# A block of two gated cross attentions on one Trainium2 core: the mask matmuls of the second attention write only their own keys, and the last keys' mask travels with the negated maximum

## The chip, the cores and the metric

The kernel runs on one core of a Trainium2 chip, as one program. TensorE (PE) multiplies matrices and writes its results to PSUM, which has eight banks; VectorE (DVE), ScalarE (ACT) and GpSimd (POOL) do the rest of the arithmetic; SyncE (SP) mostly issues transfers. Each engine works through its own instruction queue in order, and waits for the others through semaphores. The metric is the device time of one execution, in microseconds (us). A profile of one execution shows when each instruction ran.

## The reference

The input `x` has 4 batches of 1024 tokens with 256 channels; the context has 4 batches of 77 keys. Four layers follow each other, each added to `x` with a gate: a cross attention, a mixture of experts, a second cross attention with 16 heads of 16 channels, and a self attention over the 1024 tokens in two classes of tokens. The second cross attention, which the change touches, is

```python
energy = jnp.einsum('bqhd,bkhd->bhqk', q, k)             # q from the normed x, k and v from the context
energy = jnp.where(mask, energy, jnp.float32(-1e+20))    # mask: 1 x 1 x 1024 x 77, the same for every batch and head
attn = jax.nn.softmax(energy / np.sqrt(HEAD), axis=-1)
out = jnp.einsum('bhqk,bkhd->bqhd', attn, v).reshape(N, Lq, EMBED)
return out @ Wo.T + bo
```

The last layer normalises queries and guides, splits tokens into two classes by a similarity (`sim > 0.9` after scaling with the minimum and the maximum over all batches and tokens), and lets each token attend to the keys of its own class.

## The kernel before

There are two stages. The first holds everything up to the end of the second cross attention, and also the queries, keys and values of the last layer, which go to memory as `q_d`, `k_d` and `v_d`. The second is the attention of the last layer: 16 units (4 batches by 4 groups of heads), in which the scores' maxima (`ps_m` L1649, `nm` L1656), the scores (`sc` L1685, `p` L1693) and the weighted sums (`av` L1703) run interleaved. Its order is written out by hand.

The order of the first stage is made by `Plan`. Each step is added with an estimated cost for every engine that may run it, the steps it comes after, the ring buffers it takes and those it gives back. `Plan.run` then builds the program greedily: of all steps whose predecessors are done it takes the one with the least start plus lateness, where the start is worked out from the estimated costs, and it chooses the engine where there is a choice (ACT or DVE for most copies out of PSUM). The table `LATENESS` gives the lateness of some steps, by name and engine. So a changed cost moves not only its own step: it can move every later one, on every queue. The projections to keys (`keys_of`, through `store`, L695) and values (`values_of`, L711) of the last layer carry a lateness of 300, and so fill gaps of PE.

The second cross attention is `by_heads(b, m)`: one call for each pair of token tiles (256 tokens), 16 calls in all. The four row groups of 32 partitions (`r`) hold two heads each in either half of the channels (`c`), and each row group has its own PSUM bank. A call does, among other things:

- `score` (L1046 and L1056), once for each of the two tiles: into four banks of 128 tokens by 308 columns (4 heads by 77 keys) go the mask first, and then the products of queries and keys. The mask is laid down by matmuls whose stationary operand is `bias1_t`, the transposed mask values (0, or minus 2^100) of 32 keys; the moving operand `key_of` says which key each of the 32 rows stands for. There are three blocks of keys (32, 32 and 13), so three matmuls for each of the four banks, and each of the twelve writes all 308 columns.
- `greatest_` (L1069): DVE takes the negated maximum over the keys of each head.
- `split` (L1086 to L1089) and `turn_parts` (L1094): the negated maxima are split into a high and a low bf16 part and turned into rows, 8 of the 32 in each row group; the others are zero. `parts_out` copies them from PSUM to `nmt` as bf16, on ACT or DVE (L238).
- `score_t` (L1121), once for each half of the channels: the transposed scores, 77 keys by 256 tokens, in four banks. Five matmuls accumulate in each place: the product of keys and queries, the three blocks of the mask, and the negated maximum (`pick2` by `nmt`).
- `exps` (L1126), `weigh1` (L1133), the denominators' way through memory (`den`, `inv_d`, `rin`, L1172 to L1190), the division, the output projection (L1199), and then for the last layer a layer norm, `queries` (L1234), a power on POOL (L1280) and the storing of the queries.

`store` splits its result in two (a copy to `stage`, L238, and the rest by DVE, L671) and sends it to memory; `stage` has two buffers. After the last call `classes_by_token` finds the minimum and the maximum of `sim` and the classes (L1312 to L1377), and `prepare` fetches the rows of the first unit (L206), for which POOL blanks the buffers once batch 0 and batch 1 no longer use them (L1403, L1407).

The masks are made ready once, near the start, by `masks` (L566) and turned by L578; `picks` (L597 to L603) builds `key_of` and `pick2`.

Of the kernel before, what the change touches and what calls it, by code (L numbers as in the profile page):

```python
# [19 lines left out]
P = 128  # L20
# [28 lines left out]
class Plan:  # L49
# [22 lines left out]
        ("split", "DVE", 0): 150,  # L72
        ("<lambda>", "DVE", 0): 150,
        ("k_rows", "POOL", 1500): 300,
        ("parts_out", "ACT+DVE", 0): 600,
        ("sums_", "DVE", 1000): 0,
        ("all_rows", "DVE", 0): 0,
        ("q_rows", "POOL", 0): 1000,
# [81 lines left out]
def block_kernel(ctx: ExitStack, tc: tile.TileContext, t_in: dict, out: bass.AP):  # L160
# [57 lines left out]
    with ExitStack() as abc:  # L218
# [288 lines left out]
        def head_weights():  # L507
# [55 lines left out]


            def masks(_):
                ve.tensor_scalar(bias1[:, :, 0:S2], mask1, -1.0, BIG, ALU.add, ALU.mult)  # L566
                ve.tensor_copy(ident_h, ident)

            masked = work_on(masks, {DVE: 750}, ["mask1"])
# [24 lines left out]
            def picks(_):  # L594
                fold = small.tile([P, 32], F32, name="fold", bufs=1)
                col = small.tile([P, J], F32, name="pick_c", bufs=1)
                ve.tensor_reduce(fold, ident.rearrange("p (r k) -> p k r", r=J), AX.X, ALU.add)  # L597
                for q in range(3):
                    n = min(32, S2 - 32 * q)
                    ve.tensor_copy(key_of[:, q, 32 * q : 32 * q + n], fold[:, 0:n])  # L600
                ve.tensor_reduce(col, fold[:, 0 : 2 * J].rearrange("p (n e) -> p n e", e=2), AX.X, ALU.add)
                ve.tensor_copy(pick2, bc(col, 2, S2))
                ve.tensor_reduce(mine16, fold.rearrange("p (i d) -> p i d", d=D), AX.X, ALU.add)  # L603

            done.append(work_on(picks, {DVE: 1200}, []))
# [415 lines left out]
        def by_heads(b, m, after, reads):  # L1021
# [15 lines left out]
            for i in range(2):  # L1037


                def score(_, i=i):  # L1040
                    at_ = (2 * m + i) * P
                    banks = g2["s", i] = [bank("ps_e", [P, J * S2]) for r in range(4)]
                    for q in range(3):
                        for r in range(4):
                            rows32 = slice(32 * r, 32 * r + 32)
                            pe.matmul(  # L1046
                                banks[r],
                                bias1_t[rows32, q, at_ : at_ + P],
                                bc(key_of[rows32, q], 1, J),
                                start=q == 0,  # L1050
                                stop=False,
                            )
                    for c in range(2):
                        for r in range(4):
                            rows32 = slice(32 * r, 32 * r + 32)
                            pe.matmul(  # L1056
                                banks[r][:, c * 2 * S2 : (c + 1) * 2 * S2],
                                xt[rows32, c, i * P : i * P + P],
                                kb1[rows32, b, c],
                                start=False,  # L1060
                                stop=c == 1,
                            )

                def greatest_(_, i=i):
                    if i == 0:
                        g2["nm"] = small.tile([P, 2, J, J], F32, name="nm2", bufs=2)
                    for r in range(4):
                        by_head = g2["s", i][r].rearrange("p (n k) -> p n k", k=S2)
                        ve.tensor_reduce(g2["nm"][:, i, r], by_head, AX.X, ALU.max, negate=True)  # L1069

                i1 = plan.add(score, {PE: 1180}, [xt_at] + weights[2], take=["bank"] * 4)
                users.append(i1)
                tops.append(
                    plan.add(
                        greatest_, {DVE: 1620}, [i1, *tops], take=[] if i else ["nm2"], give=[("bank", i1)]
                    )
                )
# [17 lines left out]

            def parts_out(e):
                g2["nmt"] = tmp.tile([P, NQ], BF16, name="nmt", tag="nmt", bufs=plan.size["nmt"])
                copy(e, g2["nmt"], g2["ps_nm"])

            i2 = plan.add(split, {DVE: 600}, tops, take=["parts"], give=[("nm2", tops[0])])  # L1100
            i3 = plan.add(turn_parts, {PE: 300}, [i2], take=["bank"], give=[("parts", i2)])
            i4 = plan.add(parts_out, both(375, 430), [i3], take=["nmt"], give=[("bank", i3)])
            heads = []
            for c in range(2):

# [2 lines left out]
                def score_t(_, c=c):  # L1108
                    banks = g2["st", c] = [bank("ps_st", [S2, 2, NQ]) for r in range(4)]
                    at_ = 2 * m * P  # L1110
                    for i in range(2):
                        for k in range(5):
                            for r in range(4):
                                rows32 = slice(32 * r, 32 * r + 32)
                                if k == 0:
                                    of = kb1[rows32, b, c, i], xt[rows32, c, :]
                                elif k < 4:
                                    of = key_of[rows32, k - 1], bias1_t[rows32, k - 1, at_ : at_ + NQ]
                                else:
                                    of = pick2[rows32, 2 * c + i], g2["nmt"][rows32]  # L1120
                                pe.matmul(banks[r][:, i, :], *of, start=k == 0, stop=k == 4)  # L1121

                def exps(_, c=c):
                    p = g2["p", c] = act.tile([S2, 4, 2, NQ], F32, name="pt", tag="pt", bufs=plan.size["pt"])
# [18 lines left out]
                def weigh_out(e, c=c):  # L1143
                    copy(e, g2["raw"][:, :, c, :], g2["av", c])

                i5 = plan.add(score_t, {PE: 1920}, [i4], take=["bank"] * 4)
                i6 = p_at = plan.add(exps, {ACT: 2000}, [i5], take=["pt"], give=[("bank", i5), ("nmt", i4)])
                i7 = plan.add(
                    weigh1,
# [892 lines left out]
```

## Time and profile before

| | |
|---|---|
| median of 3 runs | 1187.44 us (1185.3 to 1190.38) |
| the profiled execution | 1189.9 us, its span 1188.2 us |
| instructions | 28427 |
| PE busy | 1148.5 us (97%) |
| DVE busy | 1003.2 us (84%) |
| ACT busy | 942.4 us (79%) |
| POOL busy | 610.0 us (51%) |
| mean granted TensorE clock | 0.988 of full speed |

Busy times are unions of the instructions' spans on an engine. Matmuls are pipelined and their recorded spans overlap, so 97% does not mean that PE works at its peak; how much room PE takes up is better read from the distance between the starts of one matmul group and the next. One fp32 matmul shows as two records. A group line gives the operation, its shapes, how often it ran, busy time and mean duration, and then the idle time just ahead of it with what ended it. The chain of waits goes back from the last instruction to what released it at each step. The first stage ends, and the second begins with the first `ps_m`, between 420 and 445 us.

### The profile page before, as it was taken

The numbers are of one execution on the slowest core, as the hardware profiler recorded it, in microseconds if no ns is written. First come the engines' busy times: TensorE is split into PE (matmuls) and PEld (weight loads), VectorE is DVE, ScalarE is ACT, GpSimd is POOL, SyncE is SP. The second block draws the span as 40 slices with busy tenths as digits, with TensorE's granted clock in tenths as the row PEclk, the third lists the DMA queues.
The fourth block names the chain that finished last, engine by engine and source line by source line (L and its number), as shares of the span: only waits on it lengthen the run. The fifth ranks groups of instructions, "written<-read, shape, count | busy, mean of one in ns | idle before, by whom it ended". The sixth has DMA issues, their size and how long they took to land.

```text
span 1188.2 us, 28427 instructions
## 1 busy us (share of the span) xinstructions
PE 1148.5 (97%) x10524; PEld 626.1 (53%) x10524; DVE 1003.2 (84%) x2097; ACT 942.4 (79%) x1942; POOL 610.0 (51%) x691
## 2 busy tenths in 40 slices
PE   7999999999999989999999999999999999999998
PEld 5566776777766655444434344444344444344443
DVE  5899686686866469989999999899999899999984
ACT  4875568666666413989999999899999899999886
POOL 6454566567675631644444565443564444465531
PEclk9999999999999979999999999999999999999999
DMA  8000011111112767321123341123241123220011
GB/s 240 24 1 4 21 56 67 55 48 49 48 49 74 221 204 203 69 70 34 41 62 60 60 110 38 35 65 76 60 114 38 34 62 69 70 48 20 21 28 57
DMA packets 59589, 80.27 MB, mean 68 GB/s; under 512 B 17274, under 2 KB 42789, under 8 KB 59451
## 3 DMA queue, kind: packets, MB, share of 16 engines
q1 hardware_dynamic: 55242, 73.17, 23.0%
q0 software_dynamic: 2960, 4.19, 1.6%
q8 instruction: 83, 1.36, 0.5%
q10 hardware_dynamic: 1248, 1.10, 0.3%
q14 instruction: 56, 0.45, 0.1%
HBM read 47.39 MB, written 26.07 MB: 62 GB/s over the span
## 4 chain that ended last, share of the span: by engine, by line
PE 74%; DVE 12%; ACT 6%; DMA 3%; POOL 2%; issue 2%; SPq 1%; ACTq 0%; DVEq 0%; POOLq 0%
PE av L1703 19%; PE sc L1685 17%; PE ps_m L1649 8%; DVE nm L1656 6%; PE ps_st L1121 4%; ACT p L1693 3%; PE ps_av L1133 2%; PE ps_o L1199 2%; PE ps_q L1234 2%; PE ps_xt L781 2%; PE ps_y L990 2%; PE ps_o L1760 2%; PE ps_xb L886 1%; PE ps_rs L1579 1%; PE ps_e L1056 1%
## 5 line engine op out<-in xcount | busy, mean ns | idle before, releaser
L1656 DVE TENSOR_REDUCE nm<-ps_m 128x1 f32<-128x512 f32 x1024 | 633.0, 679 | 40.8 <-PE ps_m L1649 28.5
L1693 ACT ACTIVATE p<-sc 128x512 f32<-128x512 f32 x1024 | 541.5, 631 | 28.6 <-PE ps_m L1649 18.3
L1721 POOL TENSOR_TENSOR raw<-raw,part 128x512 f32<-128x512 f32 x213 | 272.2, 1278 | 351.9 <-ACT part L1720 340.5
L1649 PE MATMUL ps_m<-slot,slot 64*128 64x512 f32 x768 | 279.6, 450 | 2.0
L1703 PE MATMUL av<-p,v 128*32 128x512 f32 x2048 | 274.2, 607 | 0.5
L1685 PE MATMUL sc<-slot,slot 64*128 64x512 f32 x768 | 239.9, 430 | 8.6 <-ACT p L1693 5.4
L1685 PEld LDWEIGHTS sc<-slot,slot 64*128 64x128 f32 x768 | 123.8, 185 | 133.4 <-ACT p L1693 52.8
L1649 PEld LDWEIGHTS ps_m<-slot,slot 64*128 64x128 f32 x768 | 128.1, 184 | 47.2 <-ACT p L1693 32.0
L1720 ACT COPY part<-av 128x512 f32<-128x512 f32 x213 | 131.7, 619 | 21.2 <-PE av L1703 19.4
L1280 POOL TENSOR_TENSOR ss_all<-ss_all,mhalf 128x16 f32<-128x16 f32 x32 | 92.6, 2903 | 12.8 <-DVE ss_all L1251 12.8
L1649 PE MATMUL ps_m<-kt,qt 64*128 64x512 f32 x256 | 90.1, 460 | 1.7 <-DVE stage L671 1.0
L1685 PE MATMUL sc<-qt,kt 64*128 64x512 f32 x256 | 84.2, 435 | 1.8 <-DMA qt<-nmt 1.6
L1126 ACT ACTIVATE pt<-ps_st 77x512 f32<-77x512 f32 x128 | 64.2, 599 | 20.2 <-PE ps_st L1121 20.2
L1703 PEld LDWEIGHTS av<-p,v 128*32 128x32 f32 x2048 | 40.4, 108 | 72.7 <-ACT p L1693 40.9
L1685 PEld LDWEIGHTS sc<-qt,kt 64*128 64x128 f32 x256 | 42.9, 185 | 63.5 <-DVE nm L1656 35.2
L1069 DVE TENSOR_REDUCE nm<-ps_e 128x4 f32<-128x308 f32 x128 | 51.7, 469 | 14.3 <-PE ps_e L1056 14.3
L769 ACT ACTIVATE xnp<-x,shift_all,rstd_all 128x256 f32<-128x256 f32 x96 | 52.1, 605 | 11.8 <-POOL shift_all L748 9.3
L736 DVE BATCH_NORM_STATS2 bn_st<-x 128x6 f32<-128x256 f32 x128 | 51.5, 403 | 2.2 <-DMA x<-in_x 1.7
L1649 PEld LDWEIGHTS ps_m<-kt,qt 64*128 64x128 f32 x256 | 41.0, 188 | 19.7 <-ACT p L1693 8.8
L238 ACT COPY xt<-ps_xt 128x512 f32<-128x512 f32 (+1 forms) x57 | 31.7, 583 | 13.9 <-PE ps_xt L781 13.4
L745 POOL TENSOR_SCALAR rstd_all<-mv_all 128x2 f32<-128x2 f32 (+3 forms) x46 | 11.4, 247 | 59.6 <-DVE mv_all L737 47.6
L746 POOL TENSOR_TENSOR rstd_all<-rstd_all,mhalf 128x2 f32<-128x2 f32 (+3 forms) x46 | 39.3, 854 | 3.8
(324 smaller groups left out, 1722.8 us busy)
## 6 DMA issues: line engine op xcount, KB each, us to landing
slot<-k_d SPq DMA_DIRECT2D x72, 128.0 KB
slot<-q_d SPq DMA_DIRECT2D x72, 128.0 KB
q_d<-stage SPq DMA_DIRECT2D x32, 256.0 KB
k_d<-stage SPq DMA_DIRECT2D x16, 512.0 KB
v_d<-vs SPq DMA_DIRECT2D x16, 272.0 KB
v<-v_d SPq DMA_DIRECT2D x16, 272.0 KB
x<-in_x SPq DMA_DIRECT2D x8, 512.0 KB
rin<-inv_d SPq DMA_DIRECT2D x32, 128.0 KB
```

Of the source, the lines that this page charges most:

```text
L736: ve.bn_stats(st[:, i, :], X[b][:, t0 + i, :])
L769: se.activation(to[:, i, :], xb[:, t0 + i, :], AF.Identity, bias=shift[:, i : i + 1], scale=rstd[:, i : i + 1],)
L1069: ve.tensor_reduce(g2["nm"][:, i, r], by_head, AX.X, ALU.max, negate=True)
L1126: se.activation(p[:, r], g2["st", c][r], AF.Exp)
L1280: gp.tensor_tensor(ss, ss, mhalf.to_broadcast([P, H]), ALU.pow)
L1649: pe.matmul(ps, QT[u % SLOTS][r, i, t * P : t * P + P], KT[u % SLOTS][r, i, h * CH : h * CH + CH], start=True, stop=True,)
L1656: ve.tensor_reduce(nm[:, 2 * i + j // 2, t % (T // 2), h : h + 1], ps, AX.X, ALU.max, negate=True)
L1685: pe.matmul(ps, KT[u % SLOTS][r, i, t * P : t * P + P], QT[u % SLOTS][r, i, ch * CH : ch * CH + CH], start=True, stop=True,)
L1693: se.activation(p[j], ps, AF.Exp)
L1703: pe.matmul(ps[32 * j : 32 * j + 32, :], V_all[b % 2][:, at : at + 32], p[j], start=True, stop=True)
L1720: se.copy(part, ps)
L1721: gp.tensor_tensor(to, to, part, ALU.add)
```

## The change

- In `score`, each mask matmul writes only the columns of its own keys, in each of the four heads: 128, 128 and 52 columns instead of 308 three times. The cost that the plan is told goes from 1180 to 1000.
- In `score_t`, the third block of the mask is no longer a matmul of its own. The mask values of keys 64 to 76 are laid 16 columns further on, so that after the turn they stand in rows 16 to 28 of each row group, where `nmt` is zero. `parts_out` adds them to the negated maxima on the way out of PSUM, and `pick2` also holds `key_of` of the third block. One matmul then adds both. Four matmuls accumulate instead of five; the planned cost goes from 1920 to 1700.
- `parts_out` is now an addition of two tensors, for which the plan has DVE alone; the entry in `LATENESS` is renamed to match.
- `masks` takes two operations instead of one, and in `picks` a copy becomes an addition.

```diff
-        ("parts_out", "ACT+DVE", 0): 600,
+        ("parts_out", "DVE", 0): 600,
...
             def masks(_):
-                ve.tensor_scalar(bias1[:, :, 0:S2], mask1, -1.0, BIG, ALU.add, ALU.mult)
+                for of, to in ((slice(0, 64), slice(0, 64)), (slice(64, S2), slice(80, S2 + 16))):
+                    ve.tensor_scalar(bias1[:, :, to], mask1[:, :, of], -1.0, BIG, ALU.add, ALU.mult)
...
-                    ve.tensor_copy(key_of[:, q, 32 * q : 32 * q + n], fold[:, 0:n])
+                    ve.tensor_copy(key_of[:, q, 32 * q : 32 * q + n], fold[:, 16 * (q == 2) : 16 * (q == 2) + n])
...
-                ve.tensor_copy(pick2, bc(col, 2, S2))
+                ve.tensor_tensor(pick2, bc(col, 2, S2), bc(key_of[:, 2], 1, J), ALU.add)
...
                     for q in range(3):
+                        keys = slice(32 * q, min(32 * q + 32, S2))
                         for r in range(4):
                             rows32 = slice(32 * r, 32 * r + 32)
                             pe.matmul(
-                                banks[r],
+                                banks[r].rearrange("p (n k) -> p n k", k=S2)[:, :, keys],
                                 bias1_t[rows32, q, at_ : at_ + P],
-                                bc(key_of[rows32, q], 1, J),
+                                bc(key_of[rows32, q, keys], 1, J),
...
-                i1 = plan.add(score, {PE: 1180}, [xt_at] + weights[2], take=["bank"] * 4)
+                i1 = plan.add(score, {PE: 1000}, [xt_at] + weights[2], take=["bank"] * 4)
...
-                copy(e, g2["nmt"], g2["ps_nm"])
+                ve.tensor_tensor(g2["nmt"], g2["ps_nm"], bias1_t[:, 2, 2 * m * P : 2 * m * P + NQ], ALU.add)
...
-            i4 = plan.add(parts_out, both(375, 430), [i3], take=["nmt"], give=[("bank", i3)])
+            i4 = plan.add(parts_out, {DVE: 430}, [i3], take=["nmt"], give=[("bank", i3)])
...
-                        for k in range(5):
+                        for k in range(4):
...
-                                elif k < 4:
+                                elif k < 3:
                                     of = key_of[rows32, k - 1], bias1_t[rows32, k - 1, at_ : at_ + NQ]
                                 else:
                                     of = pick2[rows32, 2 * c + i], g2["nmt"][rows32]
-                                pe.matmul(banks[r][:, i, :], *of, start=k == 0, stop=k == 4)
+                                pe.matmul(banks[r][:, i, :], *of, start=k == 0, stop=k == 3)
...
-                i5 = plan.add(score_t, {PE: 1920}, [i4], take=["bank"] * 4)
+                i5 = plan.add(score_t, {PE: 1700}, [i4], take=["bank"] * 4)
```

## The prediction

> **What bounds the kernel now.** I read four views: the page, a table by stage, the chain of waits in the stretch that the change touches, and the timelines of PE and SP there. From the page (busy time, share, instructions) and the table (columns: length, busy time and instructions of PE, PEld, DVE, ACT, POOL, granted clock, DMA share, GB/s):
>
> ```profile
> PE 1148.5 (97%) x10524; PEld 626.1 (53%) x10524; DVE 1003.2 (84%) x2097; ACT 942.4 (79%) x1942; POOL 610.0 (51%) x691
> ```
> ```profile
> 90.00:385.00 295.00, 290.08 (x3756) 209.96 (x3749) 217.25 (x597) 199.78 (x438) 184.54 (x204) 0.99 0.15 47
> 385.00:431.00 46.00, 43.17 (x164) 28.52 (x163) 21.96 (x57) 16.13 (x33) 26.25 (x25) 0.96 0.74 225
> 431.00:444.00 13.00, 11.33 (x28) 6.98 (x27) 9.32 (x15) 2.82 (x6) 5.33 (x5) 0.61 0.51 173
> 444.00:1188.00 744.00, 726.10 (x6119) 326.13 (x6116) 685.49 (x1223) 665.27 (x1334) 343.53 (x358) 1.00 0.26 62
> ```
>
> All calls of the second cross attention lie in 90:385. PE is covered for 290 of 295 us there, DVE for 217 (74%), ACT for 200. From 385 to 444 transfers matter too (DMA share 0.74, then 0.51). The 744 us after that are the last layer, untouched: they move as a block with their start. Shares of the chain within 90:385, by line:
>
> ```profile
> by line: PE ps_st L1121 16.3%; PE ps_av L1133 10.0%; PE ps_o L1199 8.0%; PE ps_q L1234 7.0%; PE ps_y L990 6.9%; PE ps_xt L781 6.4%; PE ps_e L1056 3.9%; PE ps_e L1046 3.9%; PE ps_y L991 3.4%; PE ps_xb L886 2.9%; DVE nm L1069 2.8%; DMA rin<-i
> ```
>
> L1121 is 48.1 us of the chain and L1046 11.5: the shortened matmuls are on it. Nearly every step there is PE's own queue, so PE bounds this stretch. The tail, from SP's timeline and the chain (start, length):
>
> ```profile
> 410.88 3.73 SPq L206 DMA_DIRECT2D kt<-k_d  x6
> ...
> 416.65 22.09 SPq L679 DMA_DIRECT2D k_d<-stage  x8
> ```
> ```profile
> 398.30 1.74 PE ps_o L1199 x8
> ...
> 430.79 0.74 PE ps_m L1649 x2
> ...
> 444.02 2.48 DVE nm L1656 x4
> ```
>
> The last output projection ends at 400.0; the last layer's first matmul starts at 430.8. Between them eight key stores go out one every 2.76 us, and DVE's queue waits behind their `stage` copies.
>
> **The change, part by part.** Everything is set against the profiled execution (span 1188.2, 1189.9 us); its differences go onto the median, 1187.4, which is 2.5 below it. The rows used (PE's timeline; then groups with busy time and mean ns; L578 with ns min/median/max and first and last start):
>
> ```profile
> 196.15 0.61 PE L1121 MATMUL ps_st<-xt,kb 32*77 32x256 f32 x8
> 196.58 0.51 PE L1121 MATMUL ps_st<-bias_t,key_of 32*77 32x256 bf16 x12
> 196.90 0.29 PE L1121 MATMUL ps_st<-nmt,pick 32*77 32x256 bf16 x4
> 197.01 0.61 PE L1121 MATMUL ps_st<-xt,kb 32*77 32x256 f32 x8
> ```
> ```profile
> 202.23 0.59 PE L1046 MATMUL ps_e<-key_of,bias_t 32*128 32x308 bf16 x12
> 202.65 0.69 PE L1056 MATMUL ps_e<-kb,xt 32*128 32x154 f32 x16
> ```
> ```profile
> L1056 PEld LDWEIGHTS ps_e<-kb,xt 32*128 32x128 f32 x496 | 18.6, 184 | 1.1
> L238 ACT CAST nmt<-ps_nm 128x256 bf16<-128x256 f32 x10 | 3.7, 371 | 5.4 <-PE ps_nm L1094 5.4
> L238 DVE CAST nmt<-ps_nm 128x256 bf16<-128x256 f32 x6 | 2.5, 410 | 0.4 <-PE ps_nm L1094 0.4
> ```
> ```profile
> L578 PE MATMUL ps_bias<-ident_h,room x96: 219/219/229, 32.9 to 34.2; 128*32 128x128 bf16 x96
> ```
>
> *Scores by key (L1121).* From start to start, three mask groups take 196.90 - 196.58 = 0.32 us, so one takes 0.107. Sixteen calls, two halves, two tiles: 64 groups go, 6.9 us of PE.
>
> *Scores by token (L1046).* Twelve matmuls take 202.65 - 202.23 = 0.42 us. Now they stream 128, 128 and 52 columns. Floor: L578 streams 128 columns in four groups side by side, 96 matmuls starting within 1.3 us, 13.7 ns each; twelve take 0.16 and save 0.26. Ceiling: each group waits for its own weights, and the one that follows is fp32 with 0.184 of loading; then about 0.39 remain and 0.03 is saved. I take two groups at L578's pace and about 0.12 for the third, because the fp32 load starts behind it: 0.24, saving 0.18. Times 32: 5.8 us (ends 1.0 and 8.2).
>
> [...]
>
> PE loses 12.7 us in all (7.9 to 15.1).
>
> *Negated maxima (L238, DVE now).* Ten of sixteen leave ACT (371 ns) for DVE. An addition from PSUM is not among the 256-wide rows; the copy's 410 ns is the nearest, and L671's addition of 512 columns takes 691, which bounds it above. At 0.42, one call's way from maximum to scores grows by 0.05 us where it left ACT, and other PE work covers that. L1121 now waits on DVE's queue: where the addition stands behind a set of four maxima (L1069, 0.469 each), it waits 1.9 us, at most 10 x 1.9 = 19 us if PE had nothing else; but in the new order weighings, transpositions or projections stand between nearly every `ps_nm` and its scores, and I put it at nothing. In the changed program's instruction order the planner also moves copies: to DVE nine of `raw` (0.69 each), two each of `z`, `w` and `qs` and one of `stage`; away from it five of `own` and one of `vs`. DVE gains 10.7 us net and ACT loses 9.4. DVE then has 228 us in a stretch of some 283: 81%, still under PE.
>
> *Preparation.* `masks` (479 ns) and the copy of `pick2` (322 ns) become slightly longer near 23 and 5 us, under transfers and PE work: 0, at most 0.4. POOL's and SP's operations keep their number.
>
> *Order.* Here most of the gain goes. In the changed order, 13 of the last layer's projections (L695, L711, 1.73 us each) stand ahead of the last weighing (L1133), against 6 before: +12.1 us, so that step moves by only -0.6. Ahead of the last output projection they are 19 against 12, and one query pass (1.83) has moved behind it: -12.7 + 12.1 - 1.8 = -2.4, so it ends at 397.6 instead of 400.0.
>
> *The tail.* Two things can set its end. By latency: the two last query passes, four powers (L1280, 2.9 each in its group), a blanking of 1.8 and the steps to the classes come to about 26.5 us, so the first `ps_m` could start at 424. By stores: in the new order eleven stores follow the first unit's fetch, and the row additions on DVE stand behind all eleven `stage` subtractions, which needs nine finished stores; before, six of nine subtractions, needing four stores. The fetch ends 7.0 us after the last value projection of batch 1 (407.6 to 414.6). That projection now ends 7.5 us ahead of 397.6 (three key projections, a transposition and the output projection lie between), at 390.1, so the fetch ends at 397.1. Nine stores at 2.76 reach 421.9. A copy, a subtraction, the columns, their turn and two additions are 4.4: 426.3. The same sum on the old order falls 1.9 short of the row, so 428.2. The stores decide: -2.6.
>
> *Start of the last layer.* Before, three subtractions (2.1 us) and a 1.1 us wait for the second half of `kt` stood among its first 13 us, at a granted clock of 0.61. They are gone: -3.0, between 0 and -6, since what holds the clock down is not shown to go.
>
> Sum: -5.6, so 1181.8.
>
> **Rivals.**
>
> *PE bounds everything.* If the tail shortens with PE's work, all 12.7 count: 1174.7. For it: the PE lines shown above are already 69% of the chain in 90:385. Against: the stores' pace of 2.76 us is no PE time.
>
> *It doesn't do what it says, or the tail takes it.* If short groups take nearly their old time (1.0 saved) and the fetch leaves later, 0 to 2 us remain: 1186. The fp32 load of 184 ns speaks for it, L578 against it.
>
> *Slower.* In the new POOL order, six powers (L1280, 2.9 us each) stand in one run ahead of the layer norm's power of a late call of batch 3. Before, at most three stand together. If that call is ready when the run starts, it waits 17.4 us, and everything behind it: 1199. It turns the sign as measured once the wait passes 5.6 + 5.9 = 11.5 us. For it: POOL can't be passed, and the planner's own times, which placed the run, have to hold on the chip. Against: POOL is 63% busy in 90:385, and it waits for DVE's statistics, not they for it.
>
> **How the numbers follow.** A measurement tells about 0.5% (5.9 us) from no change. The forecast's case 0.45 (its own range 1177 to 1187, about half of it faster), PE-bound 0.22, nothing left 0.14, slower 0.19. That gives 0.44 faster, 0.37 same, 0.19 slower. The range takes in the PE-bound case nearly to its lower end and the lower part of the slower one: 1173 to 1194.
>
> **What the new profile would show.** L1121's bias matmuls at 512 records, and 0.75 us between its fp32 groups instead of 0.86; L1046 to L1056 at 0.24 instead of 0.42; sixteen additions to `nmt` near 0.42 on DVE; PE still above DVE in 90:385; the last L1199 ending near 397.6, the first `ps_m` near 428 with no L671 after it, `nm` steady some 5.6 us sooner. Wrong it would be if DVE took over as the bound, if rows of `rstd_all` L745 waited for POOL itself, or if the stores' pace changed.

## The result, and the profile after

The changed kernel takes 1203.93 us (median of 4 runs, 1197.96 to 1204.36), the kernel before beside it 1187.65 us (4 runs, 1185.3 to 1190.38). The ratio is 1.0125, with a 95% interval of 1.0086 to 1.0163: it is slower by 16.3 us, where 1181.8 was forecast. The profiled execution took 1204.12 us, its span is 1202.4. Lines in the changed program are shifted by one or two: L1046 is now L1048, L1056 L1058, L1069 L1071, L1121 L1123, L1133 L1135, L1199 L1201, L1234 L1236, L1280 L1282, L1649 L1651, L1656 L1658; the addition to `nmt` is L1100.

From the page after (busy time, share, instructions), and from the table by stage (length, busy time and instructions of PE, PEld, DVE, ACT, POOL, granted clock, DMA share, GB/s):

```profile
PE 1150.4 (96%) x10268; PEld 624.7 (52%) x10268; DVE 1015.3 (84%) x2118; ACT 933.5 (78%) x1922; POOL 610.7 (51%) x691
```
```profile
90.00:404.00 314.00, 303.91 (x3540) 217.90 (x3533) 230.28 (x619) 196.45 (x428) 187.96 (x205) 0.97 0.16 53
404.00:433.00 29.00, 22.11 (x78) 14.90 (x77) 13.32 (x30) 8.40 (x18) 17.63 (x20) 0.84 0.71 211
433.00:447.00 14.00, 10.02 (x33) 5.54 (x32) 7.96 (x28) 3.67 (x7) 6.12 (x4) 0.87 0.52 196
447.00:1202.00 755.00, 736.37 (x6154) 331.70 (x6153) 694.46 (x1237) 666.71 (x1337) 348.90 (x361) 0.99 0.25 62
```

PE has 256 instructions less, as it should, but the stretch with all calls of the second cross attention has grown from 295 to 314 us. DVE is busy for 230 of 314 us (73%) in it, against 217 of 295 (74%) before, so by its busy time it has not become the bound. Three moments say where the time went. The last weighing (L1133) starts at 401.0 instead of 382.2; the last output projection ends at 416.8 instead of 400.0 (+16.8); the first `ps_m` starts at 449.0 instead of 430.8, so the tail takes 32.2 instead of 30.8 (+1.4); and from there to the end of the last weighted sum it is 744.6 instead of 748.7 (-4.1). Together +14.1, and the spans differ by 14.2.

The shares of the chain of waits after, first from 90 to 404 by line, and then, piece by piece (start, length, what), from 207 to 231; and below it the same view of the kernel before at the like place:

```profile
by line: PE ps_st L1123 14.3%; PE ps_av L1135 9.4%; PE ps_q L1236 6.7%; PE ps_o L1201 6.1%; PE ps_xt L782 5.0%; DVE nm L1071 4.9%; PE ps_y L991 4.6%; PE ps_e L1058 3.6%; PE ps_s L696 3.3%; DMA rin<-inv_d 3.1%; issue 2.5%; PE ps_y L992 2.2%;
```
```profile
210.32 3.05 DMA rin<-inv_d
...
213.51 1.28 POOL o L247
...
215.42 3.32 DMA rin<-inv_d
...
218.90 1.27 POOL o L247
220.17 1.68 POOL z L1008
221.85 1.23 POOL two L247
...
223.80 0.73 POOL rstd_all L747
...
225.50 0.72 POOL rstd_all L747
...
227.19 1.19 POOL rstd_all L747
...
229.49 1.58 ACT xnp L770 x3
```
```profile
195.28 1.94 PE ps_st L1121 x48
197.22 2.04 ACT pt L1126 x4
199.26 0.04 issue
199.31 0.56 PE ps_e L1046 x9
199.87 0.53 PE ps_e L1056 x16
200.39 1.90 PE ps_av L1133 x32
```

Before, the chain between 123 and 260 us runs on PE throughout but for one exponential of 2.04 us. After, 64 of these 137 us are off PE: an exponential of 2.1 as before, and 62 in three places, 123.8 to 158.6, 170.6 to 174.2, and the one shown (207.5 to 231.1). There two products `o` wait on POOL for their divisors to come back from memory (`rin`), and behind them on the same queue stand `z`, `two` and the powers of three layer norms. PE's rows have one gap of 0.06 us meanwhile; it works on other steps. The row of the normalisations on ACT over the whole program (busy time and mean ns, then the idle time before them), first of the changed kernel and then of the one before, points the same way: 27.9 us of idle time where there were 11.8.

```profile
L770 ACT ACTIVATE xnp<-x,shift_all,rstd_all 128x256 f32<-128x256 f32 x96 | 52.1, 600 | 27.9 <-POOL shift_all L749 27.9
```
```profile
L769 ACT ACTIVATE xnp<-x,shift_all,rstd_all 128x256 f32<-128x256 f32 x96 | 52.1, 605 | 11.8 <-POOL shift_all L748 9.3
```

Call by call, the operations did what was worked out. From PE's timeline after (start, length):

```profile
200.78 0.32 PE L1048 MATMUL ps_e<-key_of,bias_t 32*128 32x128 bf16 x12
200.93 0.78 PE L1058 MATMUL ps_e<-kb,xt 32*128 32x154 f32 x16
...
217.72 0.67 PE L1123 MATMUL ps_st<-xt,kb 32*77 32x256 f32 x8
218.21 0.40 PE L1123 MATMUL ps_st<-bias_t,key_of 32*77 32x256 bf16 x8
218.43 0.29 PE L1123 MATMUL ps_st<-nmt,pick 32*77 32x256 bf16 x4
218.54 0.61 PE L1123 MATMUL ps_st<-xt,kb 32*77 32x256 f32 x8
218.97 0.40 PE L1123 MATMUL ps_st<-bias_t,key_of 32*77 32x256 bf16 x8
219.19 0.29 PE L1123 MATMUL ps_st<-nmt,pick 32*77 32x256 bf16 x4
219.30 0.61 PE L1123 MATMUL ps_st<-xt,kb 32*77 32x256 f32 x8
```

Two fp32 groups of `score_t` start 219.30 - 218.54 = 0.76 us apart (0.86 before), and a half call that stands alone takes 1.689 instead of 1.908 us in the median. In `score`, the fp32 groups start 0.15 us after the mask instead of 0.42, but then take longer themselves; the whole of it, to the next instruction, takes 0.862 instead of 1.041. At these medians, 32 x 0.219 + 32 x 0.179 = 12.7 us of PE time are saved. The sum over all 32 half calls, each from its first start to the next instruction of PE, shows less, the clock as it was: 59.2 us before, 61.4 after, and 54.0 with the changed operations in the old order (the run `e1` below). In the new order several calls stand still in their middle, as the one at 306 us below does.

The tail, from the chain after:

```profile
416.51 0.55 SPq L206
...
420.34 0.55 SPq L680
...
421.63 5.80 DMA k_d<-stage
427.46 0.58 ACT stage L238
428.05 0.28 ACT xt L238
428.38 3.99 PE ps_q L1236 x8
```

The last query pass starts at 428.38, 11.5 us after the last output projection; before, it was 7.6. Its transposed input is copied on ACT behind a copy to `stage`, which waits for a key store, which SP could issue only behind the twelve transfers of the first unit's fetch (L206). PE stands for 5.8 us ahead of it.

One part of the loss is clock. The stretch from 307 to 321 after, and the rows of PE that lead up to it:

```profile
307.00:321.00 14.00, 14.00 (x116) 9.55 (x108) 6.88 (x15) 7.75 (x21) 5.94 (x7) 0.52 0.12 40
```
```profile
304.13 0.60 PE L1123 MATMUL ps_st<-xt,kb 32*77 32x256 f32 x4
306.36 0.71 PE L1123 MATMUL ps_st<-xt,kb 32*77 32x256 f32 x3 [1.63 <-ACT qs L238]
```

About 1 us after the end of a gap of 1.63 us the granted clock went to half and stayed there for 13.7 us; 14 us at 0.52 are 6.7 us of PE lost. Sixteen matmuls of the weighing (L1135) take 1.94 us in it, and 1.07 in most places of the same execution at full clock. Of the four runs of the changed kernel the one of 1197.96 has a mean clock of 0.988, the other three (1203.8 to 1204.4) of 0.978 to 0.981, so some 6 us of the 16 come and go with the clock.

### The profile page after: what moved, and what is told of

Same layout as the page of the kernel before. It is cut to its first block, busy times and chain, and to the rows that moved or that the text cites. A ratio compares the mean times of both kernels' runs of the same rounds, so it can differ in the third digit from the quotient of the medians.

```text
span 1202.4 us, 27888 instructions
## 1 busy us (share of the span) xinstructions
PE 1150.4 (96%) x10268; PEld 624.7 (52%) x10268; DVE 1015.3 (84%) x2118; ACT 933.5 (78%) x1922; POOL 610.7 (51%) x691
## 4 chain that ended last, share of the span: by engine, by line
PE 69%; DVE 15%; ACT 5%; DMA 4%; POOL 3%; issue 2%; SPq 2%; ACTq 0%; POOLq 0%; DVEq 0%
PE av L1705 19%; PE sc L1687 16%; PE ps_m L1651 8%; DVE nm L1658 7%; PE ps_st L1123 4%; ACT p L1695 2%; PE ps_av L1135 2%; PE ps_q L1236 2%; PE ps_o L1201 2%; PE ps_o L1762 2%; PE ps_xt L782 1%; DVE nm L1071 1%; PE ps_y L991 1%; SPq L206 1%; PE ps_rs L1581 1%
## 5 line engine op out<-in xcount | busy, mean ns | idle before, releaser
L1658 DVE TENSOR_REDUCE nm<-ps_m 128x1 f32<-128x512 f32 x1024 | 632.6, 679 | 41.5 <-PE ps_m L1651 28.2
L1651 PE MATMUL ps_m<-slot,slot 64*128 64x512 f32 x768 | 280.3, 450 | 2.0
L1651 PEld LDWEIGHTS ps_m<-slot,slot 64*128 64x128 f32 x768 | 128.3, 184 | 47.6 <-ACT p L1695 31.8
L1282 POOL TENSOR_TENSOR ss_all<-ss_all,mhalf 128x16 f32<-128x16 f32 x32 | 93.5, 2935 | 42.6 <-DVE ss_all L1253 38.3
L1651 PE MATMUL ps_m<-kt,qt 64*128 64x512 f32 x256 | 90.1, 461 | 1.9 <-ACT vs L1503 1.4
L1687 PE MATMUL sc<-qt,kt 64*128 64x512 f32 x256 | 86.7, 442 | 1.2 <-DMA qt<-nmt 1.0
L770 ACT ACTIVATE xnp<-x,shift_all,rstd_all 128x256 f32<-128x256 f32 x96 | 52.1, 600 | 27.9 <-POOL shift_all L749 27.9
L1071 DVE TENSOR_REDUCE nm<-ps_e 128x4 f32<-128x308 f32 x128 | 51.6, 468 | 8.1 <-PE ps_e L1058 7.9
L1123 PE MATMUL ps_st<-xt,kb 32*77 32x256 f32 x512 | 48.5, 386 | 2.9 <-ACT qs L238 1.6
L1651 PEld LDWEIGHTS ps_m<-kt,qt 64*128 64x128 f32 x256 | 40.8, 187 | 19.5 <-ACT p L1695 8.8
L672 DVE TENSOR_TENSOR stage<-ps_s,stage 128x512 fp32r<-128x512 f32 x32 | 22.0, 687 | 23.4 <-ACT stage L238 23.2
```

The source lines that it names most:

```text
L770: se.activation(to[:, i, :], xb[:, t0 + i, :], AF.Identity, bias=shift[:, i : i + 1], scale=rstd[:, i : i + 1],)
L1123: pe.matmul(banks[r][:, i, :], *of, start=k == 0, stop=k == 3)
L1282: gp.tensor_tensor(ss, ss, mhalf.to_broadcast([P, H]), ALU.pow)
L1651: pe.matmul(ps, QT[u % SLOTS][r, i, t * P : t * P + P], KT[u % SLOTS][r, i, h * CH : h * CH + CH], start=True, stop=True,)
L1658: ve.tensor_reduce(nm[:, 2 * i + j // 2, t % (T // 2), h : h + 1], ps, AX.X, ALU.max, negate=True)
L1687: pe.matmul(ps, KT[u % SLOTS][r, i, t * P : t * P + P], QT[u % SLOTS][r, i, ch * CH : ch * CH + CH], start=True, stop=True,)
```

## The experiments

All runs are medians; each was compared with runs of the kernel before on the same chip (medians 1187.85 to 1189.6). "Path" below is the time from the first scores by token (L1056) to the last weighing (L1133) in the profiled execution, one for each run: 292.7 us before, 311.7 after, of which 6.7 are the clock just shown, so 305.0 without it. "Lost clock" is one minus the granted clock, added up over a path: 1.7 us before and 8.5 after.

### Operations or order?

`e1`: the changed operations, but the plan is told the old costs and the old choice of engine, which gives the old order (the addition runs on DVE whatever the plan says).

```diff
-        ("parts_out", "DVE", 0): 600,
+        ("parts_out", "ACT+DVE", 0): 600,
-                i1 = plan.add(score, {PE: 1000}, ...)
+                i1 = plan.add(score, {PE: 1180}, ...)
-            i4 = plan.add(parts_out, {DVE: 430}, ...)
+            i4 = plan.add(parts_out, both(375, 430), ...)
-                i5 = plan.add(score_t, {PE: 1700}, ...)
+                i5 = plan.add(score_t, {PE: 1920}, ...)
```


> All operations of the changed kernel, but the plan is told the costs of before (score 1180, score_t 1920, parts_out on ACT or DVE), so the order on every queue is that of before, except that the addition to nmt always runs on DVE. Order theory (the new order leaves PE waiting, 50.8 us of gaps over 60 ns against 28.3): the 12.7 us of mask work come off PE with nothing lost, 1175 to 1183 us. Operation theory (the addition on DVE, and what waits behind it, is what costs): still 1195 us or more. No change (1184 to 1191) would say that PE's saving is hidden by the tail.

Measured: 1184.22 us, ratio 0.9965 (0.9946 to 0.9983); path 290.3.

`e2`: the operations of the kernel before, told the new costs, so in the new order (the same lines, exchanged the other way).

> All operations of before, but the plan is told the costs of the change (score 1000, score_t 1700, the copy to nmt on DVE alone), so every queue has the order of the change. Order theory: slower than the change itself by part of the 12.7 us of mask work, 1206 to 1217 us. Operation theory: a copy instead of an addition on DVE, so about as before or a little above, 1187 to 1197 us.

Measured: 1204.67 us, ratio 1.0149 (1.0127 to 1.0172); path 312.7.

So the order costs 17 to 20 us whichever operations run in it. That does not hang on the clock: `e2` and the kernel before each lost 1.7 us of clock on their paths, and the paths are 20.0 us apart. The operations cost nothing: in medians they gain 3.6 us in the old order and 0.7 in the new one. The second number is mixed with the clock. The scores that start at 298.62 in the changed kernel start 4.1 us later in `e2` (from PE's timeline of `e2`, below); after that the changed kernel runs into its half clock, and `e2` into none on its path. The changed kernel's one run at a mean clock of 0.988 is 6.7 us below `e2`'s median.

```profile
302.73 0.69 PE L1056 MATMUL ps_e<-kb,xt 32*128 32x154 f32 x16
```

Where the rest of the 12.7 us goes in the old order can be read from the two profiled paths, by the distances from one start on PE to the next, without the gaps and weighted with the granted clock: in `e1` this work is 9.4 us less than before, the gaps are 3.9 more, and 3.1 more are lost to the clock, so 2.4 are left.

Two runs ask how firmly the new order hangs on the numbers told: 10 ns less for each score step (`{PE: 990}`, `{PE: 1690}`), and both engines for the addition with the rest as changed (`both(375, 430)`).

> The changed kernel, and the plan is told 990 and 1690 instead of 1000 and 1700 for score and score_t: the operations are the same, the order moves in places. Order theory: the time moves by several us either way (somewhere from 1185 to 1212 us), though 10 ns of told cost mean nothing. Operation theory: 1203 us within 3.

> The changed kernel with the new matmul costs, but the plan may place the addition to nmt on ACT or DVE as before; it runs on DVE in any case. A third order. Order theory: somewhere from 1178 to 1205 us, and it follows the gaps on PE in the stretch of the second attention. Operation theory: 1203 us within 3.

Measured: 1202.01 (1.0135, 1.0113 to 1.0157) and 1199.47 (1.0106, 1.0091 to 1.0121), paths 306.5 and 304.4. Both are further orders, and both are slow.

### Is it the projections pulled forward?

The new order has 13 projections of the last layer ahead of the last weighing, the old one 6. Two runs exchange only their places (the edit is shortened here): the plan is run twice, with the new and the old costs, and the projections' steps of the one are put at the places, counted in PE steps of the layers, that they have in the other.

```diff
+    def run(self):
+        new, old = self.ordered(self.work), self.ordered(told)   # told: the old costs
+        base, places = (new, old)                                # the mirror run: (old, new)
+        # steps of base without the projections', and these after as many PE steps as in places
```


> Changed operations; every step of the layers in the changed program's order, but the last layer's projections (L695, L711) moved back to the places they had before: 6 instead of 13 ahead of the last weighing, 12 instead of 19 ahead of the last output projection. Two theories of what in the new order costs about 17 us. Projection theory: seven more projections of 1.73 us stand ahead of the last weighing, 12.1 us of PE time that the chain to the last layer has to wait for, and it is not paid back because after 385 us the stores and latencies, not PE, set the pace. It expects 1184 to 1191, the last weighing near 380 and the first ps_m near 426. Step theory: what costs is the order among the layers' own steps on DVE, POOL and ACT (a run of six powers on POOL, copies moved to DVE). It expects 1198 to 1206, the last weighing at 390 or later.

> The mirror of the run above: changed operations, every step of the layers in the order of the kernel before, but the projections moved to their places in the changed order (13 ahead of the last weighing, 19 ahead of the last output projection). Projection theory: 1184 plus 12 to 17, so 1196 to 1202, with the last weighing near 392. Step theory: 1183 to 1190, with the last weighing near 380, because the projections fill time in which PE stood still (39 us of gaps in 90:378 in the run with the old order).

Measured: 1229.61 (1.0349, 1.0327 to 1.037) with the path at 318.3, and 1210.97 (1.0196, 1.018 to 1.0212) with 308.0. Each is slower than both orders that it was made from. In the second, the seven projections do cost what the projection theory said and more; in the first, taking them away does not help at all. Mixtures bring stalls of their own (their tails take 48 and 40 us instead of 31), so they do not settle it.

Four more orders, each made by what the plan is told, differ in the number of projections ahead of the last weighing. In all four the plan also takes both engines for the addition, as in `e1` (first what the changed kernel tells it, then the four):

```diff
-score {PE: 1000}, score_t {PE: 1700}, LATE = 300
+score {PE: 1000}, score_t {PE: 1920}, LATE = 300     # told_score_only: 6 ahead
+score {PE: 1180}, score_t {PE: 1700}, LATE = 300     # told_keys_only: 15 ahead
+score {PE: 1300}, score_t {PE: 2100}, LATE = 300     # told_longer_fifth_order: 6 ahead
+score {PE: 1000}, score_t {PE: 1700}, LATE = 1000    # told_projections_late: 3 ahead
```


> Changed operations; the planner is told the new 1000 ns for the scores by token (L1046), but the old 1920 ns for the scores by key and both engines for the addition, which stays on DVE. It writes a third order of the layers' steps, with 6 projections ahead of the last weighing and 12 ahead of the last output projection, and at most three powers (L1280) in one run on POOL. Projection theory: 1183 to 1191, since the count of projections is that of the order before. Step theory: any order that differs from the one before can lose; it gives no number, but 1195 or more here, with so few projections, would speak for it.

> Changed operations; the planner is told the new 1700 ns for the scores by key (L1121), but the old 1180 ns for the scores by token. A fourth order, with 15 projections ahead of the last weighing and 20 ahead of the last output projection, two and one more than the changed program, and six powers in one run. Projection theory: 1200 to 1207, since nine projections more than in the order before cost 15.6 us of PE time. Step theory: no number; 1191 or less would speak for it and against the projections.

> Changed operations, and the planner is told more than they ever took: 1300 ns for the scores by token, 2100 for the scores by key. A fifth order, with 6 projections ahead of the last weighing, 12 ahead of the last output projection, and never more than two powers in a run on POOL. If the count of projections (or the runs of powers) marks the good orders, it takes 1182 to 1188. If good and bad orders fall out without such a mark, it can lie anywhere between 1184 and 1205.

> Changed operations, told their true PE times (1000 and 1700), but the projections are told to be less urgent (their lateness 1000 instead of 300). A sixth order, with 3 projections ahead of the last weighing, 7 ahead of the last output projection, runs of up to five powers. If few projections mark a good order: the last weighing 5 us sooner than with 6, near 372 to 376, and 1179 to 1188, the upper end if the tail then has more projections than it can hide. Anywhere between 1190 and 1205 if the count of projections marks nothing.

Measured, with the path, and the tail from the last output projection's end to the first `ps_m`:

| order | ahead | us | ratio (95%) | path | tail |
|---|---|---|---|---|---|
| old (`e1`) | 6 | 1184.22 | 0.9965 (0.9946 to 0.9983) | 290.3 | 30.9 |
| score told | 6 | 1186.79 | 0.9989 (0.9978 to 0.9999) | 290.2 | 31.1 |
| longer | 6 | 1199.93 | 1.0093 (1.0058 to 1.0128) | 300.0 | 39.0 |
| projections late | 3 | 1198.73 | 1.0079 (1.0048 to 1.011) | 290.5 | 44.4 |
| keys told | 15 | 1200.70 | 1.0104 (1.0089 to 1.0119) | 313.8 | 28.4 |
| changed | 13 | 1203.93 | 1.0125 (1.0086 to 1.0163) | 311.7 | 32.2 |

The first two looked like a rule for the time, and the next two broke it: six projections can go with a slow order, and three keep the path short but are paid for in the tail, where 17 of the 24 projections are then left and the first `ps_m` waits behind the last of them. For the path alone the count does go with the order, the two mixtures aside: 290 to 300 us with 3 or 6 ahead (the 300.0 with 6.8 us of lost clock), 304 to 314 with 11 to 15 (`e4` has 11, `e5` 13). Whether the projections make a path long, or only fill what the layers' steps leave free, the count can't tell; the cuts below ask that. From PE's timeline of the run with late projections, between `kt`'s row addition on DVE and the first `ps_m`, at 0.65 of the clock from 429.79 to 437.99:

```profile
426.30 0.27 PE L1372 MATMUL ps_c<-ident,more 128*32 128x128 f32 x1
429.79 8.27 PE L696 MATMUL ps_s<-xt,w_qkv 128*128 128x512 f32 x12 [3.22 <-DVE kt L1367]
437.99 0.73 PE L1651 MATMUL ps_m<-kt,qt 64*128 64x512 f32 x4
```

### What do the layers' steps wait for in the new order?

Three cuts take work off one engine each and move nothing. Each ran in the new and in the old order.

```diff
-                    for c in range(2):      # keys_of, values_of: both halves of the sum
+                    for c in range(1):      # half_proj: the first half only
...
-                        gp.tensor_tensor(ss, ss, mhalf.to_broadcast([P, H]), ALU.pow)
+                        gp.tensor_tensor(ss, ss, mhalf.to_broadcast([P, H]), ALU.mult)     # quick_powers
...
-                        ve.tensor_reduce(g2["nm"][:, i, r], by_head, AX.X, ALU.max, negate=True)
+                        if r < 2:                                                             # half_maxima
+                            ve.tensor_reduce(g2["nm"][:, i, r], by_head, AX.X, ALU.max, negate=True)
+                        else:
+                            ve.tensor_copy(g2["nm"][:, i, r], g2["nm"][:, i, r - 2])
```


> The changed program in its own order, but every projection of the last layer (L695, L711) takes only the first half of its sum (two matmuls of 0.87 us become one; the outputs are then not the reference's). Nothing is moved. 13 projections ahead of the last weighing lose 0.87 each, 11.3 us of PE. If PE time of the projections stands 1:1 on the path (projection theory), the last weighing starts near 390 instead of 401 and the run takes 1190 to 1194. If the projections only fill time in which PE waits for DVE, POOL and ACT steps anyway (step theory), the last weighing stays at 398 or later and the run takes 1200 to 1204.

> The same cut in the run with the changed operations in the old order (1184.2). Six projections ahead of the last weighing lose 0.87 each: 5.2 us. Projection theory (PE on the path 1:1): the last weighing near 372 and 1178 to 1180. Step theory: 1182 to 1185. The difference of the two runs with halved projections, set against the 19.7 us between the runs with whole ones, gives what of the loss is projections and what is the order of the layers' own steps: 7 projections less here, so projection theory alone leaves at most 14 us, and step theory 18 or more.

> The changed program in its own order, with the query powers on POOL (L1280, 2.9 us each, up to six in a run) made a multiplication of the same size, which is shorter (the outputs are then not the reference's). If the runs of powers hold up the layer norms' powers behind them, and so the statistics, the normalisations on ACT and all that hangs on them, the run falls to 1188 to 1197. If POOL only waits (its rows show it idle before most layer norms, for DVE's statistics), it stays at 1201 to 1205.

> The same shortening in the run with the changed operations in the old order (1184.2), as its control: 1182 to 1185, since in the old order at most two powers stand ahead of a layer norm that is ready. If this falls as much as the run in the new order does, the powers are not what tells the orders apart.

> The changed program in its own order, with half of the maxima (L1069, 469 ns each) left out: the third and fourth head group copy the first two groups' maxima, 128x4 each (the outputs are then not the reference's). 64 reductions become 64 short copies near 0.1 us: DVE loses about 23 us of the 208 it is busy with ahead of the last weighing, and nothing is moved. What stays open after eight runs is on what the layers' own steps wait in the new order, since neither their projections (halved: 3.3 us) nor the powers (shortened: 6 us, part of it clock) give back the 16.5 us. If the steps wait in DVE's queue, this run falls by 8 to 20, to 1184 to 1196; if they wait for one another's results (a chain of short steps through all engines), by less than 4, to 1200 or more.

> The same cut in the run with the changed operations in the old order (1184.2), as its control. PE bounds it (halved projections came back 1:1, 4.4 of 5.2 us), so at most 3 us: 1181 to 1185. If it falls as far as the run in the new order, DVE's queue does not tell the two orders apart.

> The changed program in its own order with the three cuts at once: halved projections (-11.3 us of PE ahead of the last weighing), shortened powers on POOL and half of the maxima on DVE (-23 us); the outputs are then not the reference's. With one cut each the two orders stood 20.9, 15.2 and 12.0 us apart, with none 19.7. If the new order loses to full queues (PE, POOL, DVE in turn, one hiding behind the other), the cuts together take it to 1177 to 1186, within 10 us of the old order with the same cuts. If it loses to the sequence of the steps as such (results that come late whatever the queues hold), it stays 15 us or more behind it: 1188 to 1196.

> The same three cuts in the run with the changed operations in the old order: 1184.2 less 4.4, 1.5 and 4.0 as measured one by one, so 1172 to 1178. What is told apart is the distance to the run in the new order: 10 us or less for full queues, 15 or more for the sequence as such.

| cut | new order: us (path) | old order: us (path) | distance |
|---|---|---|---|
| none | 1203.93 (311.7; 305.0 without the clock) | 1184.22 (290.3) | 19.7 |
| half of the projections' sums | 1200.63 (309.4) | 1179.77 (284.7) | 20.9 |
| powers as multiplications | 1197.97 (305.0) | 1182.74 (286.5) | 15.2 |
| half of the maxima | 1192.20 (302.9) | 1180.21 (284.6) | 12.0 |
| all three | 1189.08 (297.2) | 1174.92 (278.4) | 14.2 |

The halved projections are the clearest. In the old order they shorten the path by 5.6 us where 5.2 were cut; 1.7 of the 5.6 are clock (5.1 us lost without the cut, 3.4 with it), and the median falls by 4.4. So most of that PE time comes back there. PE is not the only bound, though: half of the maxima, which takes nothing from PE, shortens the same path by 5.7 us (4.0 without the clock) and the median by 4.0, where at most 3 were expected. In the new order five projections lie ahead of 298 us, and 4.3 us of PE are cut; yet the scores stand where they stood, with 3.4 us of clock lost between 20 us and these scores in both executions. From PE's timeline, first of the changed kernel, then of the run with halved projections in its order:

```profile
298.62 0.78 PE L1058 MATMUL ps_e<-kb,xt 32*128 32x154 f32 x16
```
```profile
298.60 0.78 PE L1058 MATMUL ps_e<-kb,xt 32*128 32x154 f32 x16
```

So in the new order PE, busy as it is, does not bound this stretch. Nor does either other queue that was relieved alone: with quick powers these scores start 0.8 us sooner, with half of the maxima 0.9. All three cuts together move them by 6.5 us (the first scores by 2.0), so the queues do hide behind one another in part:

```profile
292.09 0.78 PE L1058 MATMUL ps_e<-kb,xt 32*128 32x154 f32 x16
```

The medians fall further with the single cuts, by 6.0 and 11.7; by the bounds set beforehand the second would speak for DVE's queue. But neither profiled execution shows the half clock between 300 and 350 us, which alone is some 6; against 305.0, the paths of 305.0 and 302.9 show 0 and 2.1 for the cuts. With all three cuts the orders are still 14.2 us apart, between the 10 that were set as the bound for full queues and the 15 for the sequence. For the paths the lost clock has to come out of both orders alike: without cuts 311.7 - 8.5 = 303.2 and 290.3 - 5.1 = 285.2, 18.0 apart; with all cuts 297.2 - 3.4 = 293.8 and 278.4, with none lost, 15.4 apart. That is an estimate from single executions, which counts all lost clock as time. By it the cuts take 9.4 us off the new order's path and 6.8 off the old one's: full queues account for a few us of what tells the orders apart, and the larger part stays with the sequence of the steps. That results which the next step needs come late, as in the stretch of the chain shown above, is a reading that fits; no run moved those steps alone.

What makes one sequence good stays open. The number of projections does not settle the time, nor do the runs of powers on POOL (five in the old order, six in the new, at most two in the slow fifth one). Nor does a chain that leaves PE: in the fast run with only the score told, 76 us of the chain between 123 and 260 are off PE, in the slow `e2` 20. That the products `o` hold up the layer norms' powers behind them on POOL is read from the chain; no run moved them.

The run `e1` is the fastest with whole results: 1184.22 us, 0.35% below the kernel before (0.17 to 0.54).

## Why the prediction was wrong, step by step

- *Scores by key* and *scores by token*: right by the median call, 6.9 and 5.8 us of PE forecast, 7.0 and 5.7 measured; on the path, where calls also stand still, it is less (below). The split of the second was wrong: the mask takes 0.15, not 0.24, and the scores behind it give 0.09 back. Twelve mask matmuls in 0.155 us, in four row groups side by side, are 12.9 ns each: all three groups go at about the 13.7 ns of L578, which the forecast gave to two of them, and the 0.12 us for the third was an estimate that did not hold.
- *Negated maxima*: right. The sixteen additions take 0.412 us in the median; DVE is at 73% of the stretch, not 81%; PE waits 2.2 us in all for the addition, which was put at nothing; and with the old operations in the new order, where a copy takes the addition's place, the time is no shorter.
- *Order*: this step failed. It took the twelve microseconds of projections that stand ahead of the last weighing in the new order and let them eat up the 12.7 that PE saved: the last output projection was to end at 397.6 and ended at 416.8. The last weighing was to move by -0.6 and moved by +18.8. By the same distances between starts on PE, the path grew by 19.0: the projections took 12.4, as forecast, but the scores gave back 6.5 instead of 12.7, the gaps grew by 5.2, the lost clock by 6.8, and other steps by 1.1. So the step priced an order by counting the work of one engine ahead of a step, and counted no wait that the new order brings. Such counting came near for the old order, where most of the halved projections' time came back. In the new order it does not hold: PE's work ahead of the last weighing could be cut by 11 us with the path 2.3 us shorter. A new order of every step on five queues is a new path, and its length was never worked out. Which waits make it long stays open.
- *Tail*: the pace of nine stores was to decide. The chain runs through the last query pass instead, which comes late, behind the fetch on SP and one store; another store, of 3.0 us, stands on the 16.6 us from there to the columns (L1363). Its length was nearly right by luck: 32.2 us from the last output projection to the first `ps_m`, where 428.2 - 397.6 = 30.6 were forecast.
- *Start of the last layer*: near in size, -4.1 for -3.0, and no subtraction stands behind the first `ps_m`, as forecast. But in the 13 us from the first `ps_m` on, the clock lost 5.1 us before and 0.9 after, which is as much as the gain; what the subtractions gave is not told apart from it.
- *Rivals*: the slower case had the sign and nearly the size, 1199, but not the cause. Shortening every one of the powers, the six in one run at 367.6 us among them, left the path at the 305.0 that the changed kernel has without its half clock. Its argument that at most three powers stand together before was miscounted; five do, from 273.2 us on (ahead of a layer norm at most three). What it said of POOL, that nothing there can be passed, is what the chain shows, with a transfer at the head of the queue (`rin`, 3.05 and 3.32 us) in place of the powers. "PE bounds everything" fell with the halved projections in the new order.
- *The signs*: 0.76 us between the fp32 groups for 0.75, 512 bias records and the 0.412 us of the additions came as said. PE stayed above DVE in busy time, and that was the wrong sign to watch.

## What to carry to other kernels

Where a planner writes the order, a cost that is told to it is a change to the whole program: separate the two by running the new operations under the old costs, which here is the best version with whole results, and the old operations under the new costs. An order can't be priced by counting the busiest engine's work ahead of a step; follow the chain through all queues with durations from the trace, or take the loss of a reshuffled order as likely as a gain. A busy engine need not be the bound: here PE was busy for 303.91 of 314 us, and with 4.3 us of its work gone the scores at 298.62 us moved by 0.02. So halve some of its work without moving anything, and see whether the milestones move. When paths of single executions are compared, take the lost clock out of both (1.7 us before and 8.5 after, here).

## What was not expected of the hardware

The granted clock fell to half after a gap of 1.63 us on PE and stayed at half for 13.7 us, while PE is busy for all 14.00 us of that stretch in the table. The gap alone does not bring it: with quick powers in the new order, the same step has a gap of 1.67 us, and the clock is at 1.00 from 300 to 350 us.

```profile
305.25 0.71 PE L1123 MATMUL ps_st<-xt,kb 32*77 32x256 f32 x3 [1.67 <-ACT qs L238]
```

Ahead of 1200 us, the other stretches at half clock in the same execution lasted 3.4 us (four of them), 6.8 and 10.2. What sets the clock down, and for how long, is not shown.

Part of a matmul group's saving came back in the group behind it: with the mask shortened by 0.27 us, the fp32 products behind it took 0.09 us longer.
